# A fixed order on VectorE with postponed small items, and a new table of pieces, in a graph-attention stack

## The chip, the cores and the metric

The kernel runs on one core of one Trainium2 chip. The metric is the device time of one execution in microseconds (us); for several executions the median is given. Besides it there is one profiled execution, whose trace shows every instruction of the engines: TensorE (PE, with its weight loads as PEld), VectorE (DVE), ScalarE (ACT), GpSimd (POOL) and the DMA issues of SyncE (SP).

## What is computed

Sixteen graphs of 1024 nodes with 128 features pass through three transformer layers whose attention is limited to neighbours by one adjacency matrix, and then through one graph-attention layer. In the shortened reference below `_L0` stands for all three transformer layers, which have the same form and their own weights.

```python
def _L0_gnn_ref(adj_matrix, h, Wq, Wk, Wv, Wo, bo, ln1_g, ln1_b, W1, b1, W2, b2, ln2_g, ln2_b):
    B, N, _ = h.shape                                   # 16, 1024, 128
    Q = (h @ Wq).reshape(B, N, NUM_HEADS, HEAD_DIM)     # 8 heads of 16
    K = (h @ Wk).reshape(B, N, NUM_HEADS, HEAD_DIM)
    V = (h @ Wv).reshape(B, N, NUM_HEADS, HEAD_DIM)
    scores = jnp.einsum('bnhd,bmhd->bhnm', Q, K) / jnp.sqrt(jnp.asarray(HEAD_DIM, jnp.float32))
    mask = (adj_matrix == 0)[None, None, :, :]
    scores = jnp.where(mask, -jnp.inf, scores)
    attn = jax.nn.softmax(scores, axis=-1)
    attn_out = jnp.einsum('bhnm,bmhd->bnhd', attn, V).reshape(B, N, OUT_DIM)
    x = h + (attn_out @ Wo + bo)
    x = _layer_norm(x, ln1_g, ln1_b)
    y = jax.nn.relu(x @ W1 + b1) @ W2 + b2
    x = _layer_norm(x + y, ln2_g, ln2_b)
    return x

def _L3_gnn_ref(x, adj, W, a_src, a_dst, ln_gamma, ln_beta):
    h = x @ W
    e = (h @ a_src)[:, :, None] + (h @ a_dst)[:, None, :]
    e = jnp.where(e >= 0, e, NEG_SLOPE * e)
    e = jnp.where(adj[None, :, :] == 0, -jnp.inf, e)
    out = jnp.einsum('bij,bjd->bid', jax.nn.softmax(e, axis=-1), h)
    return layer_norm(out + x) * ln_gamma + ln_beta
```

## The kernel before

**Blocks and steps.** A block is one graph in one transformer layer; there are 48, in groups of four graphs, so that a layer of one graph lies three blocks behind its previous layer. A block has 32 steps: two head groups (g) times two halves of the queries (qh), and in each of these four halves of a block eight steps over the tiles of keys (kt 0 to 7). A step (`score_step`, L413 to L436) makes the scores of four heads: two pairs (pp), each a PSUM tile "s" of 128x1024 from two matmuls (L423). There are three "s" tiles. For kt 2, 5 and 7 (`BOTH_ON_DVE`) VectorE adds the mask to both pairs (L433) and ScalarE takes the exponentials from the result (L445). For the other kt the first pair goes to ScalarE straight from PSUM (L430) and GpSimd multiplies by the mask (L431), and only the second pair goes through VectorE. Either reading frees the "s" tile. Four steps later (`AHEAD`) `av_step` multiplies the exponentials with the values (L450, eight matmuls) into the one PSUM tile "acc". After the eighth product of a half, `finish` transposes "acc" on VectorE (tt, L461), takes reciprocals (L463) and has GpSimd scale (L464). The first product of the next half can begin only when the transpose has read "acc". Counted from the start of a block these ends fall in steps 3, 11, 19 and 27, and the first products of the next halves in steps 4, 12, 20 and 28.

**Pieces.** All other work is cut into pieces, of which `piece()` issues at most one in a step, after the step's products. `proj_tasks` makes the next block's inputs: two transposes of x (t0), keys and queries in halves (`split`: PSUM to hi on ScalarE, L385, and the rest lo on VectorE, L386) and values (v). `post_tasks` finishes the block before: transposes of the attention on VectorE (`gather`, aT, L477, both halves in one piece `both`), output projection (`out_proj`, VectorE adds, L329, takes statistics, L322 and L324, and GpSimd normalises, L337 to L341), transposes (x1t), first and second feed-forward products (ffn1, ffn2, the latter with add, statistics and normalising). Every piece uses the same single PSUM tile "t", so that a piece can begin only when the readers of the piece before it are done. `AT` gives, for each piece, the step of the block from which it may be issued; numbers of 32 and more lie in the next block. `last_tasks` is the last layer of a graph, whose pieces have gaps in place of steps.

**Order on the engines.** TensorE and ScalarE run in the order in which the program issues their instructions (`manual_schedule`). VectorE and GpSimd are put in order by the framework's scheduler, which places an instruction marked with `soon()` ahead of others. `stack` (L403 to L410) issues 16 DMAs on SP in two lots for each block, which bring the keys and queries of a head group into the form that the scores need.

The lines that a sentence can't say as well are the table before and the issue of pieces:

```python
AT = {"proj": (3, 6, 9, 11, 14, 17, 19, 20), "post": (12, 22, 23, 25, 26, 27, 28, 30, 32, 40, 41)}
...
                waiting.append((step, e, n + AHEAD))
                av_due(n)
                piece()
                n += 1
```

Of the kernel before, what the change touches and what calls it, by code (L numbers as in the profile page):

```python
# [33 lines left out]
AT = {"proj": (3, 6, 9, 11, 14, 17, 19, 20), "post": (12, 22, 23, 25, 26, 27, 28, 30, 32, 40, 41)}  # L34
AT_END = {3: (12, 21, 22, 24, 25, 26, 27, 28, 30, 31), 2: (8, 9, 13, 14, 15, 16, 17, 18, 20, 21)}
AHEAD = 4
BOTH_ON_DVE = (2, 5, 7)
TILES = {"w": 10, "x": LANES + 1, "last": 2}
# [77 lines left out]
def fast_path(ctx: ExitStack, tc: tile.TileContext, a: dict, out: bass.AP, flag):  # L116
# [163 lines left out]

    def transpose_half(name, src, h, gain=None, bias=None):
# [44 lines left out]
    def add_and_stats(n):  # L326
        def out(ts, ps):
            with soon():
                nc.vector.tensor_add(n[0][:, ts, :], v3(ps), n[0][:, ts, :])  # L329
            stats(n, ts)  # L330
        return out
# [24 lines left out]

    def proj_tasks(m):
# [4 lines left out]
        def t0(h):  # L362
            def run():
                x = state["x", b]
                if l == 0:
# [10 lines left out]
        def split(n, h):  # L376
            def run():
# [6 lines left out]
                with soon():  # L384
                    nc.scalar.copy(hi[:, c], ps)  # L385
                    nc.vector.tensor_sub(lo[:, c], ps, hi[:, c].bitcast(F32))  # L386
            return run
# [8 lines left out]
        pieces = [t0(0), t0(1), split("Wk", 0), split("Wk", 1), split("Wq", 0), split("Wq", 1), v(0), v(1)]  # L396
        return [(2 if n in (3, 4, 5, 6) else 1, f, {0: "+w", 1: "+w", 6: "-w", 7: "-w"}.get(n, "")) for n, f in enumerate(pieces)]
# [17 lines left out]
    def score_step(step):  # L415
# [3 lines left out]
        for pp in range(2):  # L419
# [12 lines left out]
            else:  # L432
                behind["dve"] = nc.vector.tensor_add(ev, psv, m).ins  # L433
                masked.append((2 * step_no[0] + pp + (kt not in BOTH_ON_DVE), ev))
# [18 lines left out]
    def finish(g, qh, acc):  # L453

        def run():
# [4 lines left out]
            with soon():  # L460
                nc.vector.transpose(tt.rearrange("p a b -> p (a b)"), acc)  # L461
            rec = state["recs"][:, g, qh, :]
# [6 lines left out]
    def post_tasks(b, l):  # L469
# [4 lines left out]
        def gather(h):  # L474
            def run():
                s["aT", h] = half_tile("aT")
                nc.vector.transpose(s["aT", h], att[:, h].rearrange("p k g d -> p (k g d)"))  # L477
                if h == 1:
                    check_range(recs.rearrange("p g h k -> p (g h k)"))
            return run  # L480

        def out_proj(h):
            def run():
                if h == 0:
                    s["n1"] = with_stats(state["x", b])
                project([s["aT", h]], [w["Wo"]], h, add_and_stats(s["n1"]))
                normalise(s["n1"], slice(4 * h, 4 * h + 4))
            return run

        def x1t(h, alone=False):  # L490
            def run():
                x1 = s["n1"][0]
# [16 lines left out]
        def ffn2(h):  # L509
            def run():  # L510
# [4 lines left out]
                normalise(s["n2"], slice(4 * h, 4 * h + 4))  # L515
            return run

        def both():
            gather(0)()
            gather(1)()  # L520


        together = [(5, both, "+w +w"), (1, out_proj(0), "-w"), (1, out_proj(1), "-w"), (5, x1t(0), "+w"), (1, x1t(1), "+w")]
        for h in range(2):
            together += [(1, ffn1(0, h), "+w"), (1, ffn1(1, h), "+w -w")]
# [15 lines left out]
    def last_tasks(b):  # L541
# [3 lines left out]
        def xt(h):  # L545
            def run():
                w = W[L - 1]
                if h == 0:
# [65 lines left out]
        def aggregate(u):  # L614
            def run():
# [11 lines left out]
                stats(s["n"], slice(2 * u, 2 * u + 2))  # L627
                if u % 2:
                    normalise(s["n"], slice(2 * u - 2, 2 * u + 2))
                if u == 3:  # L630
                    check_range(s["col"].rearrange("p c t -> p (c t)"))
            return run

        def end():
            y = s["n"][0]
# [91 lines left out]
    def av_due(n):  # L727

        for item in [w for w in waiting if w[2] <= n]:
# [14 lines left out]
            while g == 0 and qh == 0 and last_attn:  # L744
                need(last_attn.pop())
            finish(g, qh, accs.pop(half))()
# [16 lines left out]
    with tc.manual_schedule(engines={mybir.EngineType.PE, mybir.EngineType.Activation}):  # L763
        for m, (b, l) in enumerate(blocks):
# [3 lines left out]
            for at, (g, qh, kt) in enumerate((g, qh, kt) for g, qh in order for kt in range(NT)):  # L768
# [15 lines left out]
                if m + 1 < len(blocks):  # L784
# [4 lines left out]
                    if at == (24 if m == 0 else 21):  # L789
                        need(("proj", m + 1))  # L790
# [261 lines left out]
```

## Time and profile before

| quantity | value |
|---|---|
| median of 3 executions | 3983.76 us (3979.37 to 3984.21) |
| the profiled execution's own time | 3983.09 us |
| its span, first to last instruction | 3981.2 us |
| granted TensorE clock | 0.987 |
| busy share of PE, DVE, ACT, POOL | 94%, 86%, 85%, 84% |
| blocks without any piece of the last layer, 15 to 21, each | 73.13 to 73.15 us |
| blocks with a whole last layer, 23 to 26, each | 93.7 to 99.0 us |
| the last block and what follows it | 215.9 us |

The time of a block is the distance between the first exponentials of two blocks that ScalarE takes straight from PSUM. 29 of the 48 blocks are without last-layer pieces and repeat to within a few hundredths of a microsecond; such a one is called a plain block. The blocks of a row are identical, so a gain or loss in one step of the plain block is paid some 29 times or more. Busy time of TensorE includes the tails of matmuls, of which several run side by side, so its idle time is best read from the distance between the starts of consecutive groups.

### The profile page before, as it was taken

The page shows a single profiled execution, that of the slowest core. Times are in us where ns is not written, and L with a number is a line of the kernel's source. Part 1 is how long each engine was busy: PE and PEld are TensorE (multiplying, and loading weights), DVE is VectorE, ACT ScalarE, POOL GpSimd, SP SyncE. Part 2 cuts the span into 40 slices and gives each one's busy share as a digit, 9 for nine tenths or more (in the row PEclk, how much of TensorE's full clock was granted, in tenths as well). Part 3 has the DMA queues.
Part 4 walks back from the last instruction along what each step waited for, and adds up shares of the span by engine and source line. Part 5 has one row for each costly group of instructions (what it writes and reads, how often), then busy time and mean ns, then how long its engine had stood idle before and what let it go on. Part 6 is the DMA issues. An engine that isn't in the chain of part 4 may idle for free.

```text
span 3981.2 us, 107823 instructions
## 1 busy us (share of the span) xinstructions
PE 3758.5 (94%) x44501; PEld 1558.5 (39%) x44501; DVE 3408.3 (86%) x5326; ACT 3392.8 (85%) x3961; POOL 3331.4 (84%) x3010
## 2 busy tenths in 40 slices
PE   7999999999999999999999999999999999999996
PEld 2333333344443333334444333333444433333345
DVE  7888988988888988988888898888888898898874
ACT  7999999977779999997777999999777799999860
POOL 4788888987789888988778888888877898898875
PEclk8999999999999999999999999999999999999998
DMA  6222222112222222222222222221222212222200
GB/s 163 65 65 53 55 65 63 46 48 65 56 58 57 65 65 54 54 65 55 55 55 55 65 53 56 65 64 45 55 55 55 71 46 62 65 51 58 66 8 20
DMA packets 124465, 233.13 MB, mean 59 GB/s; under 512 B 34624, under 2 KB 73792, under 8 KB 123968
## 3 DMA queue, kind: packets, MB, share of 16 engines
q1 hardware_dynamic: 123056, 225.74, 22.5%
q8 instruction: 354, 5.80, 0.6%
q14 instruction: 143, 1.17, 0.1%
q10 hardware_dynamic: 912, 0.42, 0.0%
HBM read 15.54 MB, written 8.39 MB: 6 GB/s over the span
## 4 chain that ended last, share of the span: by engine, by line
PE 61%; DVE 22%; POOL 9%; ACT 4%; issue 3%; SPq 0%; DMA 0%; DVEq 0%; ACTq 0%; POOLq 0%
PE acc L450 23%; PE t L297 19%; PE s L423 16%; DVE e L433 13%; POOL e L431 3%; POOL x L341 2%; PE t L286 2%; DVE lo L386 2%; DVE st L322 2%; ACT e L445 2%; ACT e L430 2%; DVE tt L461 1%; POOL mv L339 1%; PE s L297 1%; POOL x L345 1%
## 5 line engine op out<-in xcount | busy, mean ns | idle before, releaser
L433 DVE TENSOR_TENSOR e<-s,mask_add 128x1024 f32<-128x1024 f32 x2112 | 2493.6, 1213 | 344.6 <-PE s L423 263.7
L445 ACT ACTIVATE e<-e 128x1024 f32<-128x1024 f32 x2112 | 2203.4, 1060 | 206.1 <-DVE e L433 187.9
L431 POOL TENSOR_TENSOR e<-e,mask 128x1024 f32<-128x1024 f32 x960 | 1933.5, 2026 | 419.0 <-ACT e L430 419.0
L450 PE MATMUL acc<-e,v 128*17 128x512 f32 x12288 | 1627.8, 601 | 73.3 <-DVE tt L461 47.8
L423 PE MATMUL s<-Wq,Wk 64*128 64x512 f32 x6144 | 1185.0, 456 | 58.1 <-DVE e L433 41.3
L430 ACT ACTIVATE e<-s 128x1024 f32<-128x1024 f32 x960 | 980.8, 1022 | 227.5 <-PE s L423 226.5
L423 PEld LDWEIGHTS s<-Wq,Wk 64*128 64x128 f32 x6144 | 501.2, 185 | 1027.9 <-DVE e L433 417.1
L450 PEld LDWEIGHTS acc<-e,v 128*17 128x17 f32 x12288 | 208.6, 95 | 582.1 <-issue 452.0
L341 POOL TENSOR_SCALAR x<-x,mv 128x128 f32<-128x128 f32 x896 | 389.1, 447 | 23.5
L345 POOL TENSOR_TENSOR x<-x,ln_g 128x1024 f32<-128x1024 f32 (+1 forms) x97 | 229.5, 2367 | 25.1 <-PE t L286 22.6
L339 POOL TENSOR_TENSOR mv<-mv,half_neg 128x4 f32<-128x4 f32 x224 | 232.4, 1038 | 18.6
L297 PE MATMUL t<-hd,e 128*32 128x129 f32 x7040 | 208.2, 275 | 1.2
L329 DVE TENSOR_TENSOR x<-t,x 128x512 f32<-128x512 f32 x191 | 130.8, 685 | 86.9 <-PE t L297 86.9
L297 PEld LDWEIGHTS t<-hd,e 128*32 128x32 f32 x7040 | 194.6, 110 | 16.0 <-issue 5.0
L322 DVE BATCH_NORM_STATS2 st<-x 128x6 f32<-128x128 f32 x896 | 197.3, 280 | 3.3
L297 PE MATMUL t<-x1T,W 128*32 128x512 f32 x1520 | 198.0, 592 | 0.0
L297 PEld LDWEIGHTS t<-W,hT 128*32 128x32 f32 x6080 | 170.0, 110 | 58.5 <-issue 45.5
L297 PE MATMUL t<-W,hT 128*32 128x128 f32 x6080 | 183.4, 273 | 0.2 <-DVE x L625 0.2
L286 PE MATMUL t<-identf,x 128*128 128x128 f32 x872 | 151.0, 289 | 34.0 <-DVE lo L386 15.4
L286 PEld LDWEIGHTS t<-identf,x 128*128 128x128 f32 x872 | 92.9, 141 | 230.2 <-issue 108.3
L337 POOL TENSOR_SCALAR mv<-mv 128x4 f32<-128x4 f32 x224 | 53.0, 236 | 124.6 <-DVE mv L324 98.8
L610 DVE SCALAR_TENSOR_TENSOR e<-s,mask 128x1024 f32<-128x1024 f32 x128 | 150.3, 1214 | 5.9 <-PE s L607 5.0
(118 smaller groups left out, 2573.9 us busy)
## 6 DMA issues: line engine op xcount, KB each, us to landing
Wk<-hi SPq DMA_DIRECT2D x384, 128.0 KB
Wk<-lo SPq DMA_DIRECT2D x384, 128.0 KB
Wq<-hi SPq DMA_DIRECT2D x384, 128.0 KB
Wq<-lo SPq DMA_DIRECT2D x384, 128.0 KB
x<-in_x_dram SPq DMA_DIRECT2D x16, 512.0 KB
out_dram<-x SPq DMA_DIRECT2D x31, 256.0 KB
ai<-in_adj_dram SPq DMA_DIRECT2D x8, 512.0 KB
g_rows<-parts SPq DMA_DIRECT2D x124, 4.0 KB
```

The costliest lines, as they stand in the source:

```text
L286: nc.tensor.transpose(ps[:, t * P:(t + 1) * P], src[:, 4 * h + t, :], identf)
L297: nc.tensor.matmul(dst[j:j + SLOT, :], lhsT[:, j:j + SLOT], rhs, start=start, stop=stop)
L322: nc.vector.bn_stats(st[:, t, :], z[:, t, :])
L339: nc.gpsimd.tensor_tensor(v, v, half_neg[:, ts], OP.pow)
L341: nc.gpsimd.tensor_scalar(z[:, t, :], z[:, t, :], mv[:, t, 0:1], mv[:, t, 1:2], op0=OP.add, op1=OP.mult)
L345: nc.gpsimd.tensor_mul(z, z, rows(gain, n))
L423: nc.tensor.matmul(ps[:, r * 512:(r + 1) * 512], k[64 * r:64 * r + 64, kt * P:(kt + 1) * P], q[64 * r:64 * r + 64, q0:q0 + 512], start=Tru ...
L430: nc.scalar.activation(ev, psv, AF.Exp, scale=HD ** -0.5)
L431: behind["pool"] = nc.gpsimd.tensor_mul(ev, ev, m).ins
L433: behind["dve"] = nc.vector.tensor_add(ev, psv, m).ins
L445: nc.scalar.activation(ev, ev, AF.Exp, scale=HD ** -0.5)
L450: nc.tensor.matmul(acc[j * SLOT:j * SLOT + HD + 1, :], v_bufs[m % 2][:, kt, 2 * j + g, :], e[:, j, :], start=first, stop=last)
```

## The change

VectorE joins the engines in program order. Its small items are no longer issued where they arise: `postpone` puts them into a list `later`, and `use_spare` takes from it at the end of a step, as many as fit a budget of time: 1.4 us in a step with one mask on VectorE, 0.2 us in a step with two. `settle` forces out what a later piece needs. The lo part of a split is issued behind the first mask of the next step (`behind_masks`). The table is new, keys and values come in another order, x1t(1) stands behind the first half's ffn1, and in the steps of the first products (4, 12, 20, 28) the piece is issued ahead of the products. In steps 3, 11, 19 and 27 the table has no piece. The statistics are taken in two halves of two tiles each.

```diff
-AT = {"proj": (3, 6, 9, 11, 14, 17, 19, 20), "post": (12, 22, 23, 25, 26, 27, 28, 30, 32, 40, 41)}
-AT_END = {3: (12, 21, 22, 24, 25, 26, 27, 28, 30, 31), 2: (8, 9, 13, 14, 15, 16, 17, 18, 20, 21)}
+AT = {"proj": (4, 6, 10, 12, 13, 16, 18, 20), "post": (14, 22, 24, 25, 26, 28, 29, 30, 32, 40)}
+AT_END = {3: (14, 19, 22, 23, 24, 25, 26, 27, 28, 30), 2: (8, 9, 13, 14, 15, 16, 17, 18, 20, 21)}
 AHEAD = 4
 BOTH_ON_DVE = (2, 5, 7)
+SPARE = 1.4
+MANY = 5
...
+    later, used, behind_masks = deque(), [0.0], []
+
+    def postpone(key, cost, f, first=False, at=0):
+
+        item = key, cost, f, at
+        if head[0] or tail[0]:
+            f()
+        elif first:
+            later.appendleft(item)
+        else:
+            later.append(item)
+
+    def settle(key):
+        while any(item[0] == key for item in later):
+            later.popleft()[2]()
+
+    def use_spare(room):
+        for item in list(later):
+            if item[3] > now[0]:
+                continue
+            if used[0] + item[1] > room and (len(later) <= MANY or used[0] > 0.7):
+                break
+            later.remove(item)
+            item[2]()
+            used[0] += item[1]
+        used[0] = 0.0
...
             with soon():
                 nc.vector.tensor_add(n[0][:, ts, :], v3(ps), n[0][:, ts, :])
-            stats(n, ts)
+            used[0] += 0.69
+            half = slice(ts.start, ts.start + 2), slice(ts.start + 2, ts.stop)
+            postpone(id(n), 0.65, lambda: stats(n, half[0]))
+
+            def rest():
+                stats(n, half[1])
+                normalise(n, ts)
+            postpone(id(n), 0.65, rest)
...
                     nc.scalar.copy(hi[:, c], ps)
+
+                def rest():
                     nc.vector.tensor_sub(lo[:, c], ps, hi[:, c].bitcast(F32))
+                    used[0] += 0.68
+                if head[0]:
+                    rest()
+                else:
+                    behind_masks.append(rest)
...
-        pieces = [t0(0), t0(1), split("Wk", 0), split("Wk", 1), split("Wq", 0), split("Wq", 1), v(0), v(1)]
+        return [(1, t0(0), "+w"), (1, t0(1), "+w"), (1, split("Wk", 0), ""), (1, v(0), ""), (1, v(1), ""),
+                (1, split("Wk", 1), ""), (1, split("Wq", 0), "-w"), (1, split("Wq", 1), "-w")]
...
                 behind["dve"] = nc.vector.tensor_add(ev, psv, m).ins
+                while behind_masks:
+                    behind_masks.pop(0)()
...
+            def dve():
+                nc.vector.transpose(s["aT", h], att[:, h].rearrange("p k g d -> p (k g d)"))
+
             def run():
                 s["aT", h] = half_tile("aT")
-                nc.vector.transpose(s["aT", h], att[:, h].rearrange("p k g d -> p (k g d)"))
+                postpone(id(att), 0.69, dve, True, now[0] + 3)
...
-        together = [(5, both, "+w +w"), (1, out_proj(0), "-w"), (1, out_proj(1), "-w"), (5, x1t(0), "+w"), (1, x1t(1), "+w")]
+        together = [(1, both, "+w +w"), (1, out_proj(0), "-w"), (1, out_proj(1), "-w")]
         for h in range(2):
-            together += [(1, ffn1(0, h), "+w"), (1, ffn1(1, h), "+w -w")]
+            together += [(1, x1t(h), "+w"), (1, ffn1(0, h), "+w"), (1, ffn1(1, h), "+w -w")]
...
-    with tc.manual_schedule(engines={mybir.EngineType.PE, mybir.EngineType.Activation}):
+    with tc.manual_schedule(engines={mybir.EngineType.PE, mybir.EngineType.Activation, mybir.EngineType.DVE}):
...
-                    if at == (24 if m == 0 else 21):
+                    if at == (24 if m == 0 else 22):
                         need(("proj", m + 1))
+                        while behind_masks:
+                            behind_masks.pop(0)()
                         stack(m + 1, 0)
...
                 waiting.append((step, e, n + AHEAD))
+                begins = waiting[0][2] <= n and waiting[0][0][3] == 0
+                if begins:
+                    piece()
                 av_due(n)
-                piece()
+                if not begins:
+                    piece()
+                use_spare(0.2 if kt in BOTH_ON_DVE else SPARE)
                 n += 1
```

In the last layer's `aggregate` the statistics and the normalising after them are postponed in the same way, at a cost of 0.65 each after 0.87 for its own VectorE work, and `settle` stands ahead of each reader (`t0`, `x1t`, `xt`, `end`, and the finish of the first half of a block for the attention). When the loop ends, what is left in `later` is issued, and from then on items are issued at once.

## The prediction

> **What bounds the kernel now.** I read the page's busy shares first, then the chain of waits, then the sums for one plain block, then that block's timeline.
>
> ```profile
> PE 3758.5 (94%) x44501; PEld 1558.5 (39%) x44501; DVE 3408.3 (86%) x5326; ACT 3392.8 (85%) x3961; POOL 3331.4 (84%) x3010
> ...
> PE 61%; DVE 22%; POOL 9%; ACT 4%; issue 3%; SPq 0%; DMA 0%; DVEq 0%; ACTq 0%; POOLq 0%
> ```
>
> TensorE bounds most of it, but VectorE holds 22% of the chain, and no engine has much room.
>
> ```profile
> 1409.61:1482.76 73.15, 70.70 (x722) 25.93 (x720) 65.13 (x97) 69.28 (x79) 64.64 (x57) 1.00 0.23 59
> ```
>
> A plain block takes 73.15 us: PE busy 70.70, DVE 65.13, ACT 69.28, POOL 64.64. From the starts of PE's groups, a step without stall takes 0.66 for the scores and 0.98 for the products, 1.64; a piece adds 0.86 (keys, queries, ffn1), 0.88 (values, out_proj), 0.58 (t0, x1t) or 1.79 (ffn2). Hence 32 x 1.64 + 8 x 0.86 + 4 x 0.88 + 4 x 0.58 + 2 x 1.79 = 68.8. The remaining 4.4 us are stalls, and all that the change can win. Two kinds of them in the timeline:
>
> ```profile
> 1486.76 0.71 DVE L461 STREAM_TRANSPOSE tt<-acc 128x512 f32<-128x512 f32 x1
> 1487.61 1.05 PE L450 MATMUL acc<-e,v 128*17 128x512 f32 x8 [0.56 <-DVE tt L461]
> ```
>
> PE waits for the transpose of "acc". By distances this costs 0.31 in step 4, 0.64 in 12 and 0.63 in 20: 1.58 a block.
>
> ```profile
> 1517.29 0.73 PE L423 MATMUL s<-Wq,Wk 64*128 64x512 f32 x4
> 1517.50 0.69 DVE L329 TENSOR_TENSOR x<-t,x 128x512 f32<-128x512 f32 x1 [1.16 <-PE t L297]
> 1518.23 0.87 DVE L322 BATCH_NORM_STATS2 st<-x 128x6 f32<-128x128 f32 x4
> 1519.02 0.36 DVE L324 BATCH_NORM_AGGREGATE mv<-st 128x2 f32<-128x6 f32 x4
> 1519.29 4.59 DVE L433 TENSOR_TENSOR e<-s,mask_add 128x1024 f32<-128x1024 f32 x4
> ...
> 1521.67 0.50 PE L423 MATMUL s<-Wq,Wk 64*128 64x512 f32 x2 [0.59 <-DVE e L433]
> ```
>
> Add and statistics after ffn2 put off step 1's mask and step 2's two masks; step 3's scores wait for an "s" tile: 0.86. Smaller stalls of this kind (0.13 and 0.76 in steps 14 to 17, 0.58 around the statistics after out_proj(1)) and 0.23 for GpSimd's normalising ahead of x1t(1) make up nearly all of the rest. Now a place where the scheduler's order pays:
>
> ```profile
> 1532.75 1.93 PE L297 MATMUL t<-W,hT 128*32 128x128 f32 x64
> 1533.57 1.29 DVE L477 STREAM_TRANSPOSE aT<-A 128x512 f32<-128x512 f32 x2
> 1534.79 0.66 DVE L329 TENSOR_TENSOR x<-t,x 128x512 f32<-128x512 f32 x1
> ```
>
> Both aT transposes stand ahead of the add that waits for ffn2(1), although their piece is issued after it. They fill time in which VectorE would only wait.
>
> [...] the four masks above start only behind the statistics. So a waiting add holds all behind it, and the order of issue decides. [...]
>
> **The change, part by part.** Durations of the plain block, as distances on the engine: mask 1.15 and its "s" tile free 1.23 after its start; lo 0.60; aT 0.60; add 0.73 ahead of its statistics, 0.61 otherwise; a half of the statistics 0.56 (half of 1.06, with 0.03 for the cut); tt with reciprocal 0.91, and products can go 0.85 after tt begins. A single mask can begin 0.87 after the step's first matmul, the first of two 0.60. I follow the new order by hand, times from the start of step 1.
>
> Steps 1 to 7: add at 0.21, first half of the statistics 0.94, mask of step 1 at 1.50, second half 2.65, masks of step 2 at 3.21 and 4.36, mask of step 3 at 5.51, tt at 6.66, mask of step 4 at 7.57 (before: 7.26). It is the same work: step 3's scores wait until 4.44 (before 4.38). t0(0), moved from step 3 to 4, covers tt, but ScalarE's exponentials (0.90 to 0.95 each, two a step against PE's 1.64) hold an "s" tile for 0.42 in step 4. Step 8 begins at 14.07; before it was 13.91. The 0.31 of tt is won and lost again.
>
> Steps 8 to 12: ffn2(1) ends at 17.50. The fixed order issues the add in step 8 ahead of aT, so VectorE waits out ffn2, and then everything comes at once: add 17.71, aT 18.32, mask of 9 at 18.92, aT 20.07, statistics 20.67, masks of 10 at 21.23 and 22.38, mask of 11 at 23.53, lo of Wk(0) at 24.68, tt at 25.28. Step 11 waits 0.49 for an "s" tile. In step 12 the value piece goes first and needs "t", which lo frees at 25.45, while PE is there at 24.43: 1.02. Those 1.5 us replace tt's 0.64; the two aT that lost their cover are 1.2 of them.
>
> Steps 13 to 31: out_proj(0) in step 14 puts its add and half of the statistics ahead of step 15's two masks: 0.68 in step 16. In step 20 the mask of 19 and lo come ahead of tt, and Wq(1) waits 0.50 for "t". In step 21 lo stands between two masks, and in 22 add and statistics come ahead of the masks of 23: step 24 waits 1.04. tt in 20 and 28 is covered (in 28 the piece's 0.58 and the scores' 0.66 reach 62.89, tt is done at 62.88), and x1t(1) at 28 in place of 25 saves the 0.23 for GpSimd.
>
> Sum: 0.83 + 0.42 + 0.10 + 0.08 + 0.49 + 1.02 + 0.68 + 0.50 + 1.04 = 5.2 us of stalls in place of 4.4, a block of 73.9 to 74.0, so +0.8. Ends of this sum: each of nine waits may be 0.1 smaller or larger, -0.1 to +1.7.
>
> At nothing: two more instructions of a cut are none (the same statistics). The lot of DMAs moved from step 21 to 22: its 16 issues of some 0.6 us on SP end about 10 us later, and ten steps of over 2 us are their cover; without it step 0 would wait for the rest, about 2 us. GpSimd's normalising comes one to four steps later; x of ffn2 is read three blocks later, x1 four steps later (norm 3.1 us against some 9 us). GpSimd keeps its free order. Exponentials and products are the same.
>
> Last-layer blocks (12, at 93.7 to 99.0): the trace of before has stalls of about 10 us in the block at 2006 (1.73 and 1.58 for the scores of two steps around `nodes`, 0.86 and 0.87 where a transpose waits for "t" behind lo). They are on both sides: statistics after `aggregate` no longer stand ahead of masks, but VectorE sits behind an aggregate of 3.68 on PE. I take +0.4 each, half the plain block's, bounds -2 and +3. The end, where DVE is busy 13 to 24 of 30 to 40 us: 0, bounds -5 and +8.
>
> Total: 29 x 0.8 + 5 x 0.8 (blocks 1, 10, 22, 34 and 46, of 71.8 to 78.4, taken as plain) + 12 x 0.4 = 32. The profiled execution took 3983.09, its span 3981.2; 3983 + 32 = 4015. The median is 0.7 above it, so 4016.
>
> **Rivals.** (1) Faster: the cover of tt counts in full and the waits for "t" behind lo don't arise, since VectorE does not fall behind. Its place is step 9: if aT or the statistics come later or in the wait for ffn2, lo is done in time. 34 x 1.58 = 54: 3930. For it: four tt ends a block and the piece of 0.58 to 1.79 is enough; PE floor 68.8. Against: VectorE has 7.7 us of work in a row from the add at 17.71 to the end of lo at 25.45, and PE only 6.9 from the end of ffn2(1) to the value piece. It decides if that row is under 6.9. (2) No change: gains and waits cancel, 3984; for it, steps 1 to 7, where the limit is work that stays. (3) Much slower: the fixed order also loses in the last layer, VectorE waiting for each of 48 aggregates in the loop with some 0.9 of fill lost (half the statistics and a lo or aT), 4016 + 43 = 4059. Against: PE is the bound there by far. That the order isn't what the program says would show as aT ahead of the add; then it is rival 1 or 2.
>
> **How the numbers follow.** Forecast 0.52 (own range 3992 to 4042, from 0.2 to 1.5 a block with the rest at its middle), rival 1 0.25, rival 2 0.11, rival 3 0.12. 0.2% is 8 us, about what a measurement can tell. Slower takes the forecast and rival 3 and little of 2: 0.66; faster 0.25; same 0.09. The range goes up over rival 3's middle, to 4062, and down to 3945, leaving out the better part of rival 1.
>
> **What would show it.** Plain blocks of 73.3 to 74.6; VectorE idle until the add of ffn2(1), aT behind it; a value piece that waits for lo in step 12, Wq(1) in 20; scores of step 24 that wait for a mask; no product that waits for tt. Plain blocks under 73 would prove the sum wrong, most likely in steps 9 to 12.

## The result and the profile after

The changed kernel takes 4151.8 us, the median of four executions (4144.11 to 4154.81); the kernel before took 3981.86 alongside (3979.37 to 3984.21). The ratio is 1.0424, with a 95% interval of 1.0406 to 1.0442: 4.2% slower, where 0.8% was forecast. The profiled execution took 4150.18, its span is 4148.4, the granted TensorE clock 0.980.

From the page of the changed kernel, first its busy shares, then three rows of its costliest groups (count, busy time and mean ns of one; then the idle time just ahead of the group and what ended it):

```profile
PE 3833.4 (92%) x44501; PEld 1549.9 (37%) x44501; DVE 3448.8 (83%) x5326; ACT 3377.7 (81%) x3961; POOL 3336.6 (80%) x3010
...
L480 DVE TENSOR_TENSOR e<-s,mask_add 128x1024 f32<-128x1024 f32 x2112 | 2492.2, 1213 | 368.9 <-PE s L470 316.2 <-ACT e L494 36.8 <-POOL mv L375 5.7
L499 PE MATMUL acc<-e,v 128*17 128x512 f32 x12288 | 1633.4, 603 | 11.0 <-POOL e L478 10.1 <-DVE tt L510 0.5
L470 PE MATMUL s<-Wq,Wk 64*128 64x512 f32 x6144 | 1227.0, 461 | 133.0 <-DVE e L480 106.9 <-ACT e L477 13.7 <-DVE e L665 6.6
```

The instruction counts of PE and VectorE are those of before, so no work was added. (12288 matmuls of 603 ns on the mean keep PE busy for 1633.4 us in all, so several do run side by side.) The change does what it says: products waited 47.8 us for the transpose tt before, and 0.5 now. But idle time ahead of the scores rose from 58.1 (41.3 of it ended by VectorE's mask) to 133.0 (106.9). The wait went from one PSUM tile to another, and grew.

A plain block, by the sums of a stretch (length, then busy PE, PEld, DVE, ACT, POOL, granted clock, DMA share, GB/s):

```profile
1493.14:1568.11 74.97, 71.59 (x724) 25.54 (x720) 65.94 (x97) 68.91 (x80) 64.68 (x57) 1.00 0.23 57
```

It takes 75.0 us in place of 73.15, with the same clock. Adding up blocks by kind (starts of blocks as before) says where the 167.2 us of span came from: 29 plain blocks +54.7 (+1.89 each), the four blocks 10, 22, 34 and 46, in which a last layer begins, +43.4 (+10.84 each), the twelve with a whole last layer +47.7 (+3.97 each), the last block and what follows +18.3, the first two blocks the rest, 3.1. So two thirds lie outside the plain blocks.

**The plain block's own timeline.** VectorE in steps 8 to 12, from the add that ends the second ffn2:

```profile
1512.90 0.69 DVE L358 TENSOR_TENSOR x<-t,x 128x512 f32<-128x512 f32 x1 [1.09 <-PE t L326]
1513.51 0.70 DVE L526 STREAM_TRANSPOSE aT<-A 128x512 f32<-128x512 f32 x1
1514.13 1.19 DVE L480 TENSOR_TENSOR e<-s,mask_add 128x1024 f32<-128x1024 f32 x1
1515.24 0.69 DVE L526 STREAM_TRANSPOSE aT<-A 128x512 f32<-128x512 f32 x1
1515.86 0.44 DVE L351 BATCH_NORM_STATS2 st<-x 128x6 f32<-128x128 f32 x2
1516.22 0.30 DVE L353 BATCH_NORM_AGGREGATE mv<-st 128x2 f32<-128x6 f32 x2
1516.44 3.49 DVE L480 TENSOR_TENSOR e<-s,mask_add 128x1024 f32<-128x1024 f32 x3
1519.85 0.68 DVE L428 TENSOR_TENSOR lo<-t,hi 128x512 fp32r<-128x512 f32 x1
1520.44 0.71 DVE L510 STREAM_TRANSPOSE tt<-acc 128x512 f32<-128x512 f32 x1
```

VectorE waits 1.09 us for ffn2 with both aT behind the waiting add, although GpSimd had written A by 1505.11: the add held up what stood behind it. From the add to the start of tt it is 7.54 us, and the order is the predicted one, item by item. What PE pays at the end of that row, in step 12:

```profile
1519.98 0.50 PE L470 MATMUL s<-Wq,Wk 64*128 64x512 f32 x2 [0.34 <-DVE e L480]
1520.58 1.08 PE L326 MATMUL t<-Wv,xT 128*32 128x128 f32 x32
1521.48 1.04 PE L499 MATMUL acc<-e,v 128*17 128x512 f32 x8
```

The value piece starts with the end of lo, which frees "t" (1520.53). Of the step's stall of 0.80 us, 0.51 had already gone into a wait for an "s" tile (first line; the step's second pair of scores starts 0.85 after the first, where 0.34 is usual). The two waits overlap, and the one for "t" ends last. No product waits for tt, because other waits already hold PE for longer.

**Blocks 10, 22, 34 and 46.** Block 22 of the changed kernel as sums of a stretch, with the columns as above:

```profile
1793.36:1882.31 88.95, 78.10 (x795) 28.76 (x787) 68.67 (x102) 72.89 (x93) 70.86 (x59) 0.96 0.20 50
```

The same block, in the same view, of the kernel before:

```profile
1734.62:1811.89 77.27, 72.98 (x797) 28.00 (x793) 67.19 (x102) 72.45 (x92) 69.64 (x59) 1.00 0.23 56
```

It is 11.7 us longer, of which PE is busy for 5.1, at a lower clock. The timeline of the changed kernel shows where the time goes, in steps 25 and 26:

```profile
1856.01 0.69 DVE L358 TENSOR_TENSOR x<-t,x 128x512 f32<-128x512 f32 x1
1857.61 0.24 POOL L373 TENSOR_SCALAR mv<-mv 128x4 f32<-128x4 f32 x1
1859.23 2.00 POOL L478 TENSOR_TENSOR e<-e,mask 128x1024 f32<-128x1024 f32 x1
1861.22 1.75 POOL L377 TENSOR_SCALAR x<-x,mv 128x128 f32<-128x128 f32 x4
1861.73 1.77 PE L315 MATMUL t<-identf,x 128*128 128x128 f32 x4 [4.14 <-POOL x L377]
1864.58 1.91 PE L499 MATMUL acc<-e,v 128*17 128x512 f32 x8
1866.27 1.93 PE L326 MATMUL t<-x1T,W 128*32 128x512 f32 x8
```

Here the last layer's pieces, which have gaps in place of due steps, compete with the block's own for the one piece of a step, and theirs come first. With out_proj(0) due at 14 in place of 12, a last-layer piece that is due at 13 goes ahead of it. The two out_proj come only in steps 22 and 24, and the transposes x1t(0) follow in step 25. They need what GpSimd normalises, GpSimd needs the statistics, those are postponed, and GpSimd's queue has a mask multiply of 2.00 in between. PE stands for 4.14 us, in each of the four blocks alike. After it the same kinds of group take 1.8 to 1.9 us where they took 0.66 to 1.05 elsewhere. The three stretches around it:

```profile
1855.00:1861.70 6.70, 2.59 (x44) 1.10 (x39) 4.55 (x15) 3.33 (x4) 5.97 (x7) 1.00 0.03 5
1861.70:1871.00 9.30, 9.06 (x44) 2.58 (x44) 3.97 (x4) 5.44 (x6) 5.40 (x11) 0.63 0.02 4
1871.00:1879.00 8.00, 7.76 (x64) 2.52 (x60) 5.30 (x6) 7.66 (x10) 7.93 (x5) 1.00 0.00 1
```

The granted clock is 0.63 for 9.3 us and then full again. At full clock that work takes about 0.63 x 9.3 = 5.9, an estimate; so 3.4 us come on top of the 4.14. The low clock follows a long wait elsewhere too: at the end of the kernel a wait of 3.10 us is followed by 6.4 us at 0.52. How long a wait has to be for that is not shown.

Some of the difference is work that only changed its place. The first eight matmuls of the last layer's `edges` fall into step 31 of these four blocks, and fell into the block after them before. That step takes 1.4 us longer for it, so 1.4 of the +10.84 is no loss; the next block has that much less.

**The end.** In the last block the changed kernel's timeline shows a chain of the same kind:

```profile
3980.95 0.71 DVE L510 STREAM_TRANSPOSE tt<-acc 128x512 f32<-128x512 f32 x1
3986.47 0.24 POOL L373 TENSOR_SCALAR mv<-mv 128x4 f32<-128x4 f32 x1
3991.90 0.63 POOL L514 TENSOR_TENSOR A<-tt,recs 128x256 f32<-128x256 f32 x1
3992.56 0.71 DVE L526 STREAM_TRANSPOSE aT<-A 128x512 f32<-128x512 f32 x1 [6.48 <-POOL A L514]
```

GpSimd scales A 10 us after the transpose tt was done, with normalising and mask multiplies ahead of it in the queue; VectorE waits 6.48 us, and PE's out_proj behind it 5.9. But the kernel before has this chain too:

```profile
3828.09 0.69 DVE L461 STREAM_TRANSPOSE tt<-acc 128x512 f32<-128x512 f32 x1
3837.77 0.63 POOL L464 TENSOR_TENSOR A<-tt,recs 128x256 f32<-128x256 f32 x1
3838.43 0.71 DVE L477 STREAM_TRANSPOSE aT<-A 128x512 f32<-128x512 f32 x1 [2.56 <-POOL A L464]
```

Its A comes 9.0 us after tt, and PE waits 4.2 us for the normalising and 1.3 for aT. In the changed kernel PE waits 2.3 for a mask multiply, 5.9 for aT and 3.1 for normalising. From this tt to the next one it is 36.5 us in place of 27.5, which is half of the end's +18.3; the other half is spread over the rest.

### The profile page after: what moved, and what is told of

It is laid out like the page before. It is cut to its first block, busy times and chain, and to the rows that moved or that the text cites. A ratio compares the mean times of both kernels' runs of the same rounds, so it can differ in the third digit from the quotient of the medians.

```text
span 4148.4 us, 107816 instructions
## 1 busy us (share of the span) xinstructions
PE 3833.4 (92%) x44501; PEld 1549.9 (37%) x44501; DVE 3448.8 (83%) x5326; ACT 3377.7 (81%) x3961; POOL 3336.6 (80%) x3010
## 5 line engine op out<-in xcount | busy, mean ns | idle before, releaser
L499 PE MATMUL acc<-e,v 128*17 128x512 f32 x12288 | 1633.4, 603 | 11.0 <-POOL e L478 10.1
L470 PE MATMUL s<-Wq,Wk 64*128 64x512 f32 x6144 | 1227.0, 461 | 133.0 <-DVE e L480 106.9
L326 PE MATMUL t<-hd,e 128*32 128x129 f32 x7040 | 207.7, 275 | 11.8 <-DVE lo L428 11.3
L351 DVE BATCH_NORM_STATS2 st<-x 128x6 f32<-128x128 f32 x896 | 211.6, 278 | 3.9
L560 ACT ACTIVATE hT<-t,b 128x512 f32<-128x512 f32 x190 | 133.8, 704 | 13.2 <-PE t L326 13.2
```

The source lines that it names most:

```text
L326: nc.tensor.matmul(dst[j:j + SLOT, :], lhsT[:, j:j + SLOT], rhs, start=start, stop=stop)
L351: nc.vector.bn_stats(st[:, t, :], z[:, t, :])
L470: nc.tensor.matmul(ps[:, r * 512:(r + 1) * 512], k[64 * r:64 * r + 64, kt * P:(kt + 1) * P], q[64 * r:64 * r + 64, q0:q0 + 512], start=Tru ...
L499: nc.tensor.matmul(acc[j * SLOT:j * SLOT + HD + 1, :], v_bufs[m % 2][:, kt, 2 * j + g, :], e[:, j, :], start=first, stop=last)
```

## The experiments

Each time is that of one execution, unless a ratio is given. The plain blocks of one execution lie within 0.1 us of each other in the kernel before and within 0.7 in the other runs (1.5 in `mask_first_old_table`), and each figure is the mean of 29, 4 or 12 blocks, so stages can be compared even so; the end is a single stretch. Its kernel before, measured alongside, was 3983.84, 3981.12, 3982.26 or 3983.71. The table gives each stage's difference to before in us (plain, the four blocks and the last-layer blocks: each). The 1.4 us of moved work are not in the four blocks of `order_old_table`, `proj_at_12`, `ahead_only`, `ahead_t0_at_4`, `split_earlier`, `mask_first_old_table` and `ffn2_at_31`; in those of the other runs they are.

| run | time | plain | 10, 22, 34, 46 | last layer | end |
|---|---|---|---|---|---|
| changed kernel | 4151.8 | +1.89 | +10.84 | +3.97 | +18.3 |
| order_old_table | 4270.38 | +3.81 | +4.48 | +11.12 | +22.9 |
| table_alone | 4028.93 | +0.66 | +0.95 | +1.32 | +2.9 |
| free_order | 4049.44 | +0.38 | +7.46 | +1.92 | +0.5 |
| proj_at_12 | 4099.8 | +1.29 | +4.74 | +2.89 | +23.7 |
| stats_now | 4153.24 | +3.09 | +4.53 | +3.88 | +11.8 |
| at_step_6 | 4184.2 | +2.20 | +11.31 | +5.76 | +18.9 |
| ahead_only | 4040.06 | +1.07 | +1.26 | +1.40 | +3.4 |
| ahead_t0_at_4 | 4123.8 | +1.13 | +1.33 | +8.07 | +3.4 |
| split_earlier | 4204.04 | +3.10 | +3.79 | +6.94 | +27.1 |
| ffn1_at_27 | 4169.89 | +2.45 | +10.92 | +4.28 | +19.0 |
| fixed_plain_only | 4042.18 | +0.23 | +7.47 | +1.61 | +1.8 |
| spare_behind_mask | 4135.71 | -0.30 | +6.68 | +9.03 | +25.8 |
| spare_rc_behind_mask | 4137.08 | -0.34 | +6.64 | +8.96 | +28.2 |
| mask_first_old_table | 4241.9 | +2.74 | +1.98 | +11.0 | +32.8 |
| ffn2_at_31 | 3972.79 | -0.21 | -0.39 | -0.37 | +1.0 |
| ffn2_both_earlier | 4003.91 | -0.05 | -0.23 | +1.18 | +4.9 |

### The change taken apart

`order_old_table` is the changed kernel with the old table, the old order of pieces and none ahead of the first products:

```diff
+AT = {"proj": (3, 6, 9, 11, 14, 17, 19, 20), "post": (12, 22, 23, 25, 26, 27, 28, 30, 32, 40, 41)}
...
-                begins = waiting[0][2] <= n and waiting[0][0][3] == 0
+                begins = False
```

> VectorE in fixed order with postponed items, but the old table, the old order of pieces and every piece behind the products. Theory A (the loss in the last layer comes from the table, which lets the last layer's pieces overtake out_proj(0) when it stands at step 14): blocks 10, 22, 34 and 46 fall back from 88 us to about 78, the whole to 4050 to 4090, with the plain blocks still above 74. Theory B (the fixed order costs in every stage): these four blocks stay above 84 and the whole above 4110.

`table_alone` is the reverse: the kernel before with the new table, the new order of pieces and the rule for the first products.

> The kernel before with the new table, the new order of pieces and the piece ahead of each half's first product; VectorE in the scheduler's order, nothing postponed. Theory A: blocks 10, 22, 34 and 46 rise to 84 to 90 us as in the changed kernel, the whole is 4030 to 4090. Theory B: they stay at 77 to 79 and the whole is at or under 3985, since the waits for the transpose of acc are gone.

`free_order` is the changed kernel, postponing and all, with VectorE left to the scheduler:

```diff
-    with tc.manual_schedule(engines={mybir.EngineType.PE, mybir.EngineType.Activation, mybir.EngineType.DVE}):
+    with tc.manual_schedule(engines={mybir.EngineType.PE, mybir.EngineType.Activation}):
```

> The changed kernel with VectorE back in the scheduler's order; table, halved statistics and the later place of lo in the program stay. Theory A: the four blocks 10, 22, 34 and 46 stay at 84 or more, plain blocks come down from 75.0 to 73 to 74, the whole is 4070 to 4120. Theory B: plain blocks at 72 to 73, the four blocks under 80, the whole under 4000.

By spans the table alone costs 46 us (4027.1 against 3981.2), postponing on top of it, with the halved statistics and the later lo, 20.6 (free_order, 4047.7), and the fixed order the other 101 (4148.4): 43.5 in plain blocks, 13.5 in the four, 24.7 in the last layer and 17.8 at the end. These shares hold for this order of adding the parts. With the old table, fixed order and postponing cost 287 us together, so the parts don't simply add. Two things gain: the new table under the fixed order (4151.8 against 4270.38), and postponing in the scheduler's order, in the plain blocks (from +0.66 to +0.38) and at the end (from +2.9 to +0.5). In the plain block of `order_old_table` the two longest stalls are 1.75 us in step 12 and 1.97 in step 25, the latter about half for ScalarE's exponential and half for GpSimd's late normalising ahead of x1t. The new table, with x1t(1) in step 28, stalls 0.18 in step 25. The four blocks need two of the parts: the table alone leaves them at +0.95, with postponing they are at +7.46, and the wait for GpSimd's normalising is there in free_order too, 4.34 us.

For the last layer the waits of TensorE and VectorE in blocks 23 to 26 point to the mechanism (total us, times, longest), first in the changed kernel:

```profile
DVE col L677 <- PE t L326: 25.8, 14, 4.0
DVE x L358 <- PE t L326: 9.7, 9, 2.8
...
PE t L326 <- DVE lo L428: 6.6, 7, 1.4
...
PE s L470 <- DVE e L480: 4.0, 6, 1.7
```

and in free_order:

```profile
DVE col L677 <- PE t L326: 20.0, 13, 4.0
...
DVE x L358 <- PE t L326: 5.9, 9, 1.2
...
PE t L326 <- DVE lo L428: 2.0, 2, 1.1
...
PE s L470 <- DVE e L480: 0.7, 1, 0.7
```

In fixed order VectorE stands 9.6 us longer for `col` and the add, which wait for long products, and what lies behind comes late: PE waits 7.9 us more for lo and masks. These blocks are 10.2 us longer in sum. That is the fixed order's share; why the table and postponing cost these blocks another 1.92 each was not taken further.

`proj_at_12` brings out_proj(0) back to step 12, ahead of both values:

```diff
-AT = {"proj": (4, 6, 10, 12, 13, 16, 18, 20), "post": (14, 22, 24, 25, 26, 28, 29, 30, 32, 40)}
+AT = {"proj": (4, 6, 10, 13, 14, 16, 18, 20), "post": (12, 22, 24, 25, 26, 28, 29, 30, 32, 40)}
```

> The changed kernel with out_proj(0) at step 12 in place of 14, and the two value pieces at 13 and 14. Theory A: out_proj(0) keeps its place ahead of the last layer's first piece at 13, the four blocks 10, 22, 34 and 46 come down from 88 to 79 to 82 us, the blocks with a whole last layer by 1 to 3 each, the whole to 4070 to 4110; plain blocks lose the wait for lo in step 12 (no piece that needs t at once) and stand at 74.0 to 75.5. Theory B: the four blocks stay above 85, the whole above 4130.

The four blocks fall from +10.84 to +4.74. Without the 1.4 of moved work the place of out_proj(0) is half of their loss. In block 22 the wait for normalising is gone, and the clock stays at 1.00. Blocks 10, 22 and 34 take 81.1 us (88.0 to 88.9 in the changed kernel). Block 46 takes 85.9: its due steps stand in `AT_END`, which this edit leaves as it is. The due steps of the last block stand there too, so that the end (+23.7) tells nothing of out_proj(0)'s place. A plain block gains 0.60, as the stall of step 16 falls from 0.87 to 0.07: the add of out_proj(0) no longer stands ahead of two masks. The whole comes to 4099.8.

### What the plain block pays for

`stats_now` takes whole statistics where they arise and normalises at once; only aT and small range checks are still postponed. `at_step_6` lets aT go two steps earlier:

```diff
-                postpone(id(att), 0.69, dve, True, now[0] + 3)
+                postpone(id(att), 0.69, dve, True, now[0] + 1)
```

> The changed kernel with statistics and normalising issued at once behind their add (in add_and_stats and in aggregate), not postponed; fixed order, table and the rest stay. Theory C (in the last layer and at the end the loss is GpSimd's: postponed statistics put its normalising off, and out_proj's x1t, or the scaling of the attention, stands behind it): blocks 10, 22, 34 and 46 come down from 88 to 78 to 82, the end from 234 to 217 to 225, plain blocks rise by 0 to 1 since four tiles of statistics stand ahead of two masks again; the whole 4080 to 4130. Theory B (the fixed order itself): these blocks stay above 85 and the end above 230, the whole is at 4150 or more.

> The changed kernel with the aT transposes allowed two steps earlier, in step 6 in place of 8, where VectorE has one mask and no add. The prediction's reading (1.2 us of aT stand between the add of ffn2(1) and lo, and the value piece in step 12 waits for them): the stalls of steps 11 and 12, 0.58 and 0.80, fall to under 0.4 together, plain blocks come from 75.0 to 73.9 to 74.3, the whole to 4110 to 4125. If another wait is next in line there, plain blocks stay within 0.3 of 75.0 and the whole above 4135.

Without postponing, a plain block loses another 1.2 us: stalls of 1.12 in step 11, 1.30 in 16 and 1.54 in 24, against 0.58, 0.87 and 1.09. So postponing the statistics in halves helps the plain block, if the order is fixed. The four blocks recover over half (+4.53) and the end a third (+11.8), while the whole stays (4153.24). In block 22 PE no longer waits for normalising, though out_proj(0) still comes in step 22, and the clock stays at 1.00. So the wait of 4.14 us needs both, the overtaken out_proj and the late normalising: either edit removes it, with the slow clock behind it. At the end late normalising is paid for only in fixed order, since free_order has +0.5 there. With aT earlier, step 11 stalls 0.24 and not 0.58, but step 8 stalls 0.64 and step 12 keeps its 0.80. From the add to tt it is still 7.20 us (7.54): where aT left the row, the second half of the statistics and the range checks came in. So this run doesn't price the 1.2 us of aT that lost their cover.

`ahead_only` and `ahead_t0_at_4` add the rule for first products to the kernel before, the latter with t0(0) at step 4:

```diff
+                begins = waiting[0][2] <= n and waiting[0][0][3] == 0
+                if begins:
+                    piece()
                 av_due(n)
-                piece()
+                if not begins:
+                    piece()
```

> The kernel before with one thing of the change: in a step of a half's first product the piece is issued ahead of the products (old table, which has pieces in steps 12, 20 and 28; VectorE in the scheduler's order). The tt waits of steps 12 and 20, 0.64 and 0.63, go: plain blocks 72.0 to 72.5, the whole 3930 to 3960. If the cover makes another wait for t or an s tile of the same size, 3975 to 3990.

> As ahead_only, with t0(0) at step 4 in place of 3, so that a piece stands ahead of all four first products. If the wait for tt in step 4 is what costs there: 0.2 to 0.3 a plain block better than ahead_only, 10 us in all. If steps 1 to 7 are held by the work of VectorE and ScalarE, as the prediction reckoned: within 0.1 a plain block of ahead_only.

The rule alone costs 1.07 us a plain block. Step 12 stalls 1.24 in place of 0.64, step 20 0.55 in place of 0.63, and step 28, which had no stall, 0.46. The piece ahead covers tt, but needs "t", and that is free only when the piece before it has been read, by VectorE's lo in step 12 and by ScalarE in 20 and 28: one wait was exchanged for another that is no shorter, or hardly. With t0(0) at step 4 (`ahead_t0_at_4`) the plain block changes by 0.06, but the last-layer blocks lose 80 us. There the last layer's pieces fall into other steps: in blocks 24 to 26 one with an aggregate now takes step 12, ahead of the products, and out_proj(0) slides behind it to 13. In blocks 23 to 26 TensorE waits 9.9 us until lo has freed "t" (7.2 in `ahead_only`), 8.1 for mask multiplies (5.3), 5.8 until VectorE has read an aggregate (none) and 3.8 for normalising (none), at a mean clock of 0.97 (0.99). Which of these moves costs most was not tested.

`split_earlier` puts Wk(0) at step 9 and Wq(0) at 17, so that lo is done sooner; `ffn1_at_27` fills the empty step 27:

```diff
-AT = {"proj": (4, 6, 10, 12, 13, 16, 18, 20), "post": (14, 22, 24, 25, 26, 28, 29, 30, 32, 40)}
+AT = {"proj": (4, 6, 9, 12, 13, 16, 17, 20), "post": (14, 22, 24, 25, 26, 28, 29, 30, 32, 40)}
...
-AT = {"proj": (4, 6, 10, 12, 13, 16, 18, 20), "post": (14, 22, 24, 25, 26, 28, 29, 30, 32, 40)}
+AT = {"proj": (4, 6, 10, 12, 13, 16, 18, 20), "post": (14, 22, 24, 25, 27, 28, 29, 30, 32, 40)}
```

> The changed kernel with the pieces Wk(0) and Wq(0) one step earlier, 9 and 17 in place of 10 and 18, so that Wk(0)'s lo is issued in step 10, two steps ahead of the value piece that needs t. Theory D (lo behind the next step's first mask ends at best 0.87 + 1.15 + 0.68 + 0.1 = 2.8 us after that step began, and a piece that stands directly behind the scores of the step after it wants t after 1.64 + 0.66 = 2.3, so at least 0.5 of wait is built in): the stall of step 12, 0.80, falls under 0.2 and plain blocks come from 75.0 to 74.2 to 74.6, unless lo between the two masks of step 10 costs an s tile. Rival (VectorE is late by aT and statistics whatever the place of lo): step 12 keeps over 0.5, plain blocks at 74.8 to 75.5.

> The changed kernel with ffn1(1,0) at step 27 in place of 26: the step in front of a first product has a piece again. Theory E (a step without a piece is over in 1.64 us, less than ScalarE's two exponentials, 1.85, so the scores of step 28 wait for ScalarE to free an s tile; the table's empty steps 3, 11, 19 and 27 cause such waits): the stall of step 28, 0.45, falls under 0.15 and plain blocks to 74.5 to 74.8. Rival (the wait is tt's or t's): step 28 keeps it, plain blocks stay at 74.9 to 75.3.

Both are slower. With lo earlier, step 12 stalls only 0.31, but step 11 stalls 0.90 for a mask, and step 17, where Wq(0) now follows Wk(1) at once, 1.33 for the lo that frees "t". With ffn1 at 27, the scores of step 28 no longer wait 0.34 for ScalarE's exponential, so the empty step did cause that wait. But the stall of step 28 grows from 0.45 to 1.00: ffn1's result is read by ScalarE, and the piece of step 28 waits for that. An empty step is thus the cheaper of the two.

`fixed_plain_only` gives VectorE the fixed order in plain blocks alone, one step at a time. The scheduler still moved masks over the bounds of steps, ahead of small items, so it isn't the part of the change it was meant to be:

```diff
+                plain = 1 < m < 10 or 14 < m < 22 or 26 < m < 34 or 38 < m < 46
...
+                with (tc.manual_schedule(engines={mybir.EngineType.DVE}) if fixed else nullcontext()):
```

> The changed kernel with VectorE in fixed order in the 29 plain blocks only; in blocks with pieces of the last layer and at the end it is left to the scheduler. If the costs of the fixed order add up stage by stage: plain blocks at 74.9 to 75.2, blocks 10, 22, 34 and 46 as with the free order at 84 to 86, blocks with a whole last layer at 97.5 to 99.5 on the mean, the end 215 to 219, the whole 4085 to 4110. If the fixed order of one stage makes the next one late, the sum fails by more than 20.

It is useful for that very reason: plain blocks at +0.23, not +1.89, and what differs in VectorE's order is that masks stand ahead of statistics and of the reciprocals behind tt. (The last layer, in free order, is at +1.61.) That made a theory: the fixed order costs because small items, issued at the end of a step, stand ahead of the next step's first mask, which frees an "s" tile. `spare_behind_mask` keeps the fixed order everywhere and puts them behind that mask:

```diff
-                use_spare(0.2 if kt in BOTH_ON_DVE else SPARE)
+                spare_due[0] = True
...
+                if spare_due[0]:
+                    spare_due[0] = False
+                    use_spare(0.2 if kt in BOTH_ON_DVE else SPARE)
```

> The changed kernel with one thing moved: the postponed items that fit a step's budget are issued behind the first mask of the next step, not ahead of it. Theory F (the loss of the fixed order is that adds and statistics of a step stand ahead of the next step's mask, which is what frees an s tile; in the run in which the scheduler could move masks across the bounds of a step, plain blocks took 73.36): plain blocks come from 75.0 to 73.2 to 73.9 and the whole to 4040 to 4110. Rival (any fixed order costs, since VectorE waits at the head of its queue): plain blocks over 74.5, the whole over 4120.

VectorE's timeline in this kernel after ffn2(1) ends:

```profile
1500.81 1.29 DVE L529 STREAM_TRANSPOSE aT<-A 128x512 f32<-128x512 f32 x2
1502.03 0.65 DVE L358 TENSOR_TENSOR x<-t,x 128x512 f32<-128x512 f32 x1
1502.69 1.22 DVE L480 TENSOR_TENSOR e<-s,mask_add 128x1024 f32<-128x1024 f32 x1
1503.83 0.47 DVE L351 BATCH_NORM_STATS2 st<-x 128x6 f32<-128x128 f32 x2
```

The sums of one of its plain blocks:

```profile
1482.00:1554.90 72.90, 71.57 (x724) 25.36 (x720) 65.77 (x97) 68.99 (x79) 64.77 (x57) 1.00 0.25 59
```

The mask follows the add at once and the statistics come behind. A plain block takes 72.85 us: 2.19 less than in the changed kernel, and less than before. The stalls that masks caused fall: step 3 from 1.02 to 0.34, step 11 from 0.58 to nothing, step 16 from 0.87 to 0.13, step 24 from 1.09 to 0.38. Step 4 rises from 0.42 to 0.91, as its product waits for tt again; steps 12 and 20 keep theirs (0.84 and 0.36). The edit moved one thing more: aT, postponed too, stands ahead of the add again (first line). That can bear on steps 8 to 12, of which only step 11 gained, and `at_step_6`, which moved aT alone, gained nothing in sum. So the plain block lost by where items stand, not by a fixed order as such. But the last layer goes from +3.97 to +9.03 and the end to +25.8, so the whole gains little.

> As spare_behind_mask, and the reciprocals behind each tt, with the scaling on GpSimd after them, also wait behind the next step's first mask. Theory F: another 0.1 to 0.4 a plain block, since the mask fills the time between tt and its reciprocal; the whole 4030 to 4100. Rival: no gain over spare_behind_mask, or a loss of up to 20 in all where GpSimd's scaling comes late at the end.

The same with tt's reciprocal behind the mask too (`spare_rc_behind_mask`) changes a plain block by 0.04: nothing. With the old table and without pieces ahead of first products (`mask_first_old_table`) it is slower than the kernel before in every stage:

> The order of spare_rc_behind_mask with the old table (ffn2(0) at 31), the old order of pieces, and every piece behind the products: what a fixed order with masks ahead can do with the table that the scheduler's order had. Theory F: the fixed order with the old table cost 287 because items stood ahead of masks; plain blocks fall from 77.0 to 73.3 to 74.5, the whole from 4268 to 4030 to 4110. Rival: plain blocks stay over 75.5.

At +2.74 a plain block, items behind masks do worse without the new table and its pieces ahead; which of the two they need was not taken apart. Its longest stalls are 2.19 in step 12 and 2.10 in step 25, the latter mostly for GpSimd's normalising.

### A version that beats both

The kernel before has its longest plain stall, 0.87 us, in step 3, behind the statistics of ffn2(0). `ffn2_at_31` moves that piece one step earlier, and `ffn2_both_earlier` the second one too:

```diff
-AT = {"proj": (3, 6, 9, 11, 14, 17, 19, 20), "post": (12, 22, 23, 25, 26, 27, 28, 30, 32, 40, 41)}
+AT = {"proj": (3, 6, 9, 11, 14, 17, 19, 20), "post": (12, 22, 23, 25, 26, 27, 28, 30, 31, 40, 41)}
...
-AT = {"proj": (3, 6, 9, 11, 14, 17, 19, 20), "post": (12, 22, 23, 25, 26, 27, 28, 30, 32, 40, 41)}
+AT = {"proj": (3, 6, 9, 11, 14, 17, 19, 20), "post": (12, 22, 23, 25, 26, 27, 28, 30, 31, 39, 41)}
```

> The kernel before with one number of its table changed: ffn2(0) at step 31 in place of 32, so that its add and statistics fall in front of two steps with one mask on VectorE, not one. By the row of the timeline before, step 3's scores wait until 4.38 us after ffn2 ended; with one more step in between the wait is 0.3 in place of 0.86: plain blocks 72.4 to 72.8, the whole 3955 to 3975. If the freed time only moves to the next wait (ScalarE's in steps 4 to 7), plain blocks stay within 0.15 of 73.15, the whole 3978 to 3990.

> The kernel before with both ffn2 pieces one step earlier (31 and 39 in place of 32 and 40). If VectorE's backlog of step 8 causes the waits of steps 12 to 17, plain blocks come to 72.2 to 72.7 and the whole to 3945 to 3965. If ffn2(1) in step 7 has to wait for t, which ScalarE reads late there, plain blocks stay at 72.9 or above and the whole is at 3970 to 4000.

The first takes 3972.79 us (10 executions), a ratio of 0.9975 (0.9965 to 0.9985). Step 3 stalls 0.34 in place of 0.87. Step 4 keeps its 0.31 for tt, and step 5 now stalls 0.35 for ScalarE's exponential, so a plain block gains only 0.21, less than the 0.35 to 0.75 expected. With both moved the ratio is 1.0052 (1.0034 to 1.007): plain blocks keep 0.05 of that gain, step 7 stalls 0.18 where ffn2(1) waits until ScalarE has read "t", and the last layer and the end lose more.

## Why the prediction was off

**The direction, and the mechanism of the plain block: right.** VectorE idle until ffn2's add with both aT behind it, then one row of work up to tt: 7.57 us by the prediction, 7.54 measured. Step by step, predicted and measured stalls are: step 3 0.83 and 1.02; step 4 0.42 and 0.42; step 11 0.49 and 0.58; step 12 1.02 and 0.80; step 16 0.68 and 0.87; step 20 0.50 and 0.36; step 24 1.04 and 1.09. "In step 12 the value piece goes first and needs t, which lo frees" is what the trace shows, with a wait for an "s" tile under it that the prediction did not have. The terms for steps 12 and 20 were too large by 0.22 and 0.14, those for 3, 11, 16 and 24 too small by 0.05 to 0.19; that their sum over these seven is near (4.98 and 5.14) is partly luck.

**A plain block at +0.8: too small.** It is +1.89, just over the upper end of +1.7. Stalls are 6.1 in place of 4.3, where 5.2 was forecast. Missing are 0.27 in step 18, 0.18 in 25, and 0.45 in 28. There the text had tt covered to within 0.01, and didn't ask when ScalarE frees the "s" tile for the scores: they wait 0.34 for it. 29 times 1.1 us are 32 us of the error.

**The step that failed: "Last-layer blocks ... I take +0.4 each", "blocks 1, 10, 22, 34 and 46 ... taken as plain", "The end ...: 0".** The forecast's sum has about 8 us there (12 x 0.4 and 4 x 0.8). It was 43.4 + 47.7 + 18.3 = 109.4, of which about 101 us are error, three quarters of it all. It failed in three ways. The four blocks were priced by the plain block, though the last layer's pieces compete for the steps of the table there. And late normalising stood in the list of things at nothing: "norm 3.1 us against some 9". That cover exists in a plain block, where x1t(0) comes ten steps after out_proj(0). Where out_proj is overtaken, it comes after three, one step after out_proj(1), and the wait costs 4.14 us and, by the estimate for block 22, some 3.4 more by the clock; `proj_at_12` and `stats_now` each remove it.

The twelve last-layer blocks were put at +0.4, "half the plain block's", with bounds up to +3; they measured +3.97. The fixed order is 24.7 of their 47.7 us, and the traces point to VectorE waiting in line for long products.

The end was put at 0, with bounds of -5 and +8, and took 18.3 more. GpSimd was named as one that "keeps its free order", and what VectorE's late statistics do in GpSimd's queue was not followed. `stats_now` gives back a third of it; the cause of the rest stays open.

**Rivals.** Rival 1 (faster) named its own test, the row from the add to lo: over 6.9 us, as predicted, so it fell; tt was covered in full, and other waits took the place of its own. Rival 3 had the mechanism for the last layer: VectorE waits for long products in line. Its 43 us lie near the 47.7 measured by luck, since the fixed order is only 24.7 of these and the table with postponing the rest. It left out the four blocks and the end. (The forecast's own range, 3992 to 4042, comes to about 3996 to 4040 by the figures given for it.)

**What stays open.** Why items behind the mask, good for plain blocks, cost the last layer another 5 us a block; which of the pieces that move with t0(0) cost the 80 us of `ahead_t0_at_4`; and most of the end. A run with fixed order in plain blocks, items behind masks, and free order elsewhere was not made: `fixed_plain_only` showed that a fixed order bounded in this way is not kept.

## What to carry to other kernels

An engine's fixed order is a list of who frees what: put the instruction that frees a buffer TensorE waits for ahead of those that only fill time. In the plain block here that was worth 2.2 us of 75, but the last layer lost by the same order, so each stage has to be measured. Covering one wait is worth something only if the cover's own inputs (here the tile "t") come earlier than the wait would have ended: in `ahead_only` step 12 stalled 1.24 us in place of 0.64. When a table of due steps is changed, follow it through each kind of block, and through the queue of every engine that gets its work later, since the rare blocks can cost more than the common one (here +10.84 us each against +1.89).

## What the runs showed that I had not expected

In block 22 a wait of TensorE cost nearly twice its length: 4.14 us idle, then 9.3 us at a granted clock of 0.63 (3.4 us more by the estimate above), in which a group of eight products takes 1.91 in place of 1.05. The kernel before has such a wait at its end, 4.18 us and then 4.7 us at 0.51. Shorter waits of the changed kernel are followed by a low clock too: 3.10 us (0.52 for 6.4 us behind it), and in block 25 one of 2.97 (0.50 for 4). The plain block above, with stalls of up to 1.09 us and 6.1 in all, stands at 1.00. In between the runs show no limit: a wait of 1.18 us was followed by 4 us at 0.57 in block 13, and by 4 us at 1.00 in block 25.

Two VectorE orders with the same instructions, counts and nearly the same busy time (65.94 and 65.77 us) differ by 2.2 us a block, about 63 us over 29 plain blocks.
